# Gated linear attention and an FP4 MLP on one core: roots of norms taken on GpSimd, norms turned sooner, the causal mask selected

## The chip, the cores and the metric

The kernel runs on one core of a Trainium2 chip. A core has five engines that run side by side, each through its own list of instructions in order, and wait for one another on semaphores: TensorE (PE; its weight loads are listed apart as PEld), VectorE (DVE), ScalarE (ACT), GpSimd (POOL) and SyncE (SP), which here issues DMA transfers. The metric is the device time of the whole kernel in microseconds.

## The reference

Two pre-normed residual layers over x of 4 sequences x 512 tokens x 512 numbers:

```python
x = x + attn(layernorm(x), ...)     # gated linear attention, chunked
x = x + ffn(layernorm(x), ...)      # weights of 4 bits, 32 share a scale

def layernorm(x): return (x - mean) / sqrt(var + 1e-05)

# attn: 4 heads of 128, chunks of 128 tokens; q, k, v = x @ W + b
k = k / maximum(norm(k), 1e-12)
alpha, beta = sigmoid(x @ Walpha + balpha), softplus(x @ Wbeta + bbeta)
cla = cumsum(log(alpha + 1e-06))                    # within a chunk
decay = where(causal, exp(cla_i - cla_j), 0)
y_local = ((q @ k.T) * beta_j * decay) @ v
state = state * exp(cla_end) + (v.T @ (k * beta * exp(cla_end - cla)))
y = y_local + (q @ old state) * exp(cla)

# ffn: 512 -> 4096 -> 512
out = (gelu(x @ Wg.T) * (x @ Wu.T)) @ Wd.T
```

## The kernel before

**Tiling.** A tile is 128 tokens, which is one chunk; a sequence ("batch", b from 0 to 3) has four tiles (n from 0 to 3), so there are 16 chunks. `two_k` and `one_k` are lists of 24 and 42 fixed SBUF homes, taken and given back by name (`Homes`); PSUM has eight tiles of 128 x 512, used in rotation (`psum`).

**Order.** All is written out by hand (`manual_schedule`). The main loop (L858) goes through twelve products for each batch: four of v (`product_v`, a tile each), four of q (`product_q`, a head each), four of k (`product_k`, a tile each). After each product comes a *place*, numbered p, in which `behind(p)` (L656) issues the other work. Three places make a round for one chunk:

- p % 3 = 0: `chunk_lead` (k turned by TensorE, copied by ACT), `take_roots` (ACT's square roots of all that has been gathered), `gates_sums` once per batch, `chunk_decay`.
- p % 3 = 1: `settle` (what follows the roots on DVE), `chunk_scores`, `gates_end` once per batch, the load of the residual tile.
- p % 3 = 2: `turn` (normed tiles turned by TensorE and passed on), `gates_ln` once per batch, `chunk_sums`, and the statistics of a tile of the next batch (`first_norm`).

The chunk that a place works on is (p - 9) // 3, so chunks trail the k products. The second layer (`mlp`, a generator) goes through 35 rounds, i from 0 to 34, of 1 to 4 blocks of 128 hidden columns, batch i % 4 in turn. A block has two products of 12 matmuls (`gate_up`, L719); a round ends in `down` (L755), but for round 0, whose part is summed in round 4. Each product and each `down` is again followed by a place while attention is still going on; two of these stand between the k products of the last batch. So the last four chunks lie among the first rounds of the second layer. Round i with r = i - 3 has all four blocks from i = 3 on ("round zero", r = 0).

**A norm.** `norm` (L322) has DVE make statistics (L324, L326) and puts a root on a list. `take_roots` (L344) runs ACT's Sqrt. `settle` (L353) has DVE take the reciprocal (L331) and write the normed tile hn (L334). `turn` (L358) has TensorE transpose it (L362), and its `use` passes it on: of the first norm, ACT copies into hT (L373), from which all products read; of the second norm, ACT and DVE split it in three (L384 to L386), and SP stores the pieces in DRAM (h<-g, L388), from which each round of the second layer loads them (x<-h, L310 through `load_x`, twelve tiles per round). The second norm comes from `chunk_sums` (L646), so it passes three places from statistics to `turn`.

**k's norm.** `product_k` sums squares (ACT L448, DVE L450) and bounds them (L452); the root is again ACT's (L347); DVE takes the reciprocal (L456) and multiplies it with beta (brn, L458) and with beta and the decay to the end (kwf, L460). POOL scales v by brn (vb, L611) and k by kwf (kw, L607) in `chunk_scores`.

**Decay.** `chunk_decay` has TensorE spread a row of cla over 128 rows: `all_of` (48 x 128, ones at the rows of a chunk) times `rowsum` (48 x 512). pc (L558, if n > 0) is that alone; pm (L560) is the same with a second product added (L561) that puts -32768 where the mask is 0. ACT takes exp of pc (cd, L566), and of pm with cla_j subtracted, per head (dm, L577). POOL makes qc = q x cd (L568) and the decayed state (L585). TensorE makes scores sp (L595), DVE multiplies them into dm (L612). `chunk_sums` has TensorE add kw x v (dp, L624) to the state (DVE L626 or L628), and make yp from dm x vb (L637) and qc x old state (L639); DVE adds yp to the residual (L644).

**x of a round.** `load_x(i + 1, ...)` is issued in `last()` (L791), between the second product of a round's last block and what DVE does with it; for some rounds the first six of the twelve go out ahead, before the block numbers in `ahead` (L786): block 0 from i = 3 on, block 1 for i = 1, none for i = 2. SP's queue issues them in this order, behind the stores that they read from.

**Weights** of the second layer are unpacked on DVE and ACT (`dequant`), a step or two at a time from a queue (`unpack`), between the products.

## Time and profile before

| what | us |
|---|---|
| median of 3 runs | 1347.25 (1345.63 to 1349.15) |
| the profiled execution's own time | 1347.27 |
| its span, first to last instruction | 1345.5 |
| PE busy | 1318.1 |
| DVE, ACT, POOL busy | 983.8, 489.0, 62.0 |

In the profile, L12 is line 12 of the kernel before. `out<-in` are tiles by the program's names with numbers left out: tp_a and tp_f are the turned first and second norm, hn_a and hn_f the normed tiles. A busy time counts overlapping instructions once. "Idle <-" and the lists of waits name what an engine's wait ended on; a wait for several things is put down to the last. Matmuls are pipelined and listed with a modelled end, so the distance from one start to the next says what one costs.

### The profile page before, as it was taken

To read this page: it belongs to the slowest core of one execution; us is meant where nothing else is said; L and a number is where in the kernel's file an instruction comes from. 1 tells how busy PE (TensorE), PEld (TensorE's weight loads), DVE (VectorE), ACT (ScalarE), POOL (GpSimd) and SP (SyncE) were. 2 spreads that over 40 slices of the span, in tenths; PEclk is the share of its full clock that TensorE was granted. 3 is DMA by queue.
4 is the path that set the end of the run, shared out by engine and by line. 5 is a ranking of instruction groups with operands and counts; after the bars stand their busy time and mean duration, and the time that the engine had idled before them with its cause. 6 is when DMAs were issued, how large, how long until landed. Compare 5 with 4: busy or idle time off the path is not lost.

```text
span 1345.5 us, 17010 instructions
## 1 busy us (share of the span) xinstructions
PE 1318.1 (98%) x5828; PEld 1047.1 (78%) x5828; DVE 983.8 (73%) x1631; ACT 489.0 (36%) x855; POOL 62.0 (5%) x78
## 2 busy tenths in 40 slices
PE   8999999989999999999999999999999999999998
PEld 5576767676888888888888888888888888887886
DVE  4577766587767777777777777777778787777556
ACT  2554545544333333333333333333333333332232
POOL 0031313110000000000000000000000000000000
PEclk9999999999999999999999999999999999999999
DMA  7033334766555565556565656565656465555473
GB/s 235 24 99 105 103 94 132 264 199 213 187 164 194 176 194 180 191 181 199 177 199 185 194 178 206 185 195 173 201 175 206 156 216 172 189 172 188 149 254 129
DMA packets 173798, 236.57 MB, mean 176 GB/s; under 512 B 15760, under 2 KB 74128, under 8 KB 173712
## 3 DMA queue, kind: packets, MB, share of 16 engines
q1 hardware_dynamic: 173008, 235.20, 53.9%
q8 instruction: 46, 0.75, 0.2%
q10 hardware_dynamic: 704, 0.28, 0.1%
q14 instruction: 40, 0.33, 0.1%
HBM read 183.00 MB, written 52.43 MB: 175 GB/s over the span
## 4 chain that ended last, share of the span: by engine, by line
PE 89%; DVE 4%; ACT 3%; DMA 2%; issue 1%; POOL 1%; SPq 0%; POOLq 0%; DVEq 0%; ACTq 0%
PE pa L719 33%; PE p_d L755 25%; PE pb L719 16%; PE pq L428 4%; PE pva L403 2%; PE pvb L410 2%; PE pk L440 2%; DMA x<-h 1%; PE yp L637 1%; PE sp L595 1%; PE dp L624 1%; PE yp L639 1%; DMA h<-g 1%; ACT L349 0%; ACT sq L448 0%
## 5 line engine op out<-in xcount | busy, mean ns | idle before, releaser
L719 PE MATMUL pa<-x,wgu 128*128 128x512 f32 x2048 | 509.4, 390 | 0.9 <-DMA x<-h 0.7
L719 PEld LDWEIGHTS pa<-x,wgu 128*128 128x128 f32 x2048 | 385.1, 188 | 82.3 <-DMA x<-h 2.5
L755 PE MATMUL p_d<-wd,i 128*128 128x512 f32 x1536 | 358.3, 391 | 3.7 <-DVE i L740 2.5
L755 PEld LDWEIGHTS p_d<-wd,i 128*128 128x128 f32 x1536 | 288.7, 188 | 67.2 <-DVE i L740 3.5
L725 ACT ACTIVATE t<-pb 128x512 f32<-128x512 f32 x256 | 151.3, 591 | 352.6 <-PE pb L719 350.1
L719 PE MATMUL pb<-x,wgu 128*128 128x512 f32 x1024 | 275.0, 390 | 0.6 <-DMA x<-h 0.4
L726 DVE TENSOR_TENSOR t<-pa,t 128x512 f32<-128x512 f32 x256 | 176.5, 689 | 104.4 <-ACT t L725 99.1
L719 PEld LDWEIGHTS pb<-x,wgu 128*128 128x128 f32 x1024 | 192.3, 188 | 41.8 <-DMA x<-h 1.4
L768 DVE SCALAR_TENSOR_TENSOR acc<-p_d,acc 128x512 f32<-128x512 f32 x136 | 93.3, 686 | 109.3 <-PE p_d L755 102.0
L738 ACT ACTIVATE i<-t 128x512 fp32r<-128x512 f32 x128 | 81.0, 633 | 196.3 <-DVE t L735 194.8
L730 ACT ACTIVATE t<-t 128x512 f32<-128x512 f32 x128 | 81.1, 633 | 154.1 <-DVE t L726 154.1
L740 DVE TENSOR_TENSOR i<-t,i 128x512 fp32r<-128x512 f32 x128 | 88.2, 689 | 24.1 <-ACT i L738 22.6
L769 DVE TENSOR_TENSOR acc<-acc,p_d 128x512 f32<-128x512 f32 x136 | 93.6, 688 | 15.6 <-PE pa L719 1.4
L735 DVE SCALAR_TENSOR_TENSOR t<-t,t 128x512 f32<-128x512 f32 x128 | 88.6, 692 | 4.4
L741 DVE SCALAR_TENSOR_TENSOR i<-i,t 128x512 fp32r<-128x512 f32 x128 | 87.7, 685 | 0.2 <-DMA h<-g 0.2
L440 PE MATMUL pk<-wk,hT 128*128 128x512 f32 x128 | 57.6, 592 | 0.0
L428 PE MATMUL pq<-hT,wq 128*128 128x512 f32 x128 | 57.5, 593 | 0.0
L428 PEld LDWEIGHTS pq<-hT,wq 128*128 128x128 f32 x128 | 23.7, 190 | 23.9 <-issue 23.4
L440 PEld LDWEIGHTS pk<-wk,hT 128*128 128x128 f32 x128 | 23.5, 190 | 23.6 <-issue 23.4
L211 DVE SCALAR_TENSOR_TENSOR wgu<-wgu,w_gu 128x1024 fp32r<-128x1024 f32 x32 | 39.4, 1232 | 2.4 <-ACT wgu L208 2.4
L202 DVE SCALAR_TENSOR_TENSOR w_gu<-i_gu,sc_gu 128x1024 f32<-128x1024 f16 x32 | 39.7, 1240 | 0.0
L214 DVE TENSOR_TENSOR wgu<-wgu,wgu 128x1024 fp32r<-128x1024 f32 x32 | 39.5, 1234 | 0.0
(133 smaller groups left out, 911.6 us busy)
## 6 DMA issues: line engine op xcount, KB each, us to landing
x<-h SPq DMA_DIRECT2D x420, 256.0 KB
acc<-acc SPq DMA_DIRECT2D x256, 256.0 KB
h<-g SPq DMA_DIRECT2D x48, 256.0 KB
x<-in_x SPq DMA_DIRECT2D x16, 256.0 KB
pk_gu<-in_gate_p SPq DMA_DIRECT2D x32, 128.0 KB
sc_gu<-in_gate_s SPq DMA_DIRECT2D x64, 64.0 KB
pk_gu<-in_up_p SPq DMA_DIRECT2D x32, 128.0 KB
sc_gu<-in_up_s SPq DMA_DIRECT2D x64, 64.0 KB
```

Source lines behind the costliest of these rows:

```text
L428: nc.tensor.matmul(pq, f32(wq[k // 2])[:, k % 2, h * P : (h + 1) * P], f32(hT[b][k // 2])[:, k % 2, :], start=(k == 0), stop=(k == KC - 1),)
L440: nc.tensor.matmul(pk, f32(hT[b][k // 2])[:, k % 2, n * P : (n + 1) * P], f32(wk[k // 2])[:, k % 2, :], start=(k == 0), stop=(k == KC - 1),)
L719: nc.tensor.matmul(o, w3[j][:, k % 2, c * P : (c + 1) * P], x[j * KC + k], start=(j == js[0] and k == 0), stop=(j == js[-1] and k == KC - 1),)
L725: nc.scalar.activation(f32(t), pb, AF.Copy, scale=-1.0 / ONE_E)
L726: nc.vector.tensor_tensor(f32(t), pa, f32(t), ALU.add)
L730: nc.scalar.activation(f32(g), f32(g), AF.Gelu_apprx_tanh, scale=ONE_E)
L735: nc.vector.scalar_tensor_tensor(f32(u), f32(g), ONE_E, f32(u), ALU.mult, ALU.mult)
L740: nc.vector.tensor_tensor(il, f32(u), f32(ih), ALU.subtract)
L741: nc.vector.scalar_tensor_tensor(im, f32(ih), ONE_E, f32(u), ALU.mult, ALU.subtract)
L755: nc.tensor.matmul(o, inter[i][j][:, n * P : (n + 1) * P], wd[ms[i] // 2][j][:, ms[i] % 2, :], start=(i == 0 and j == js[0]), stop=(i == L ...
L768: nc.vector.scalar_tensor_tensor(a, pas[2 * n], ONE_E, a, ALU.mult, ALU.add)
L769: nc.vector.tensor_tensor(a, a, pas[2 * n + 1], ALU.subtract)
```

## The change

The roots move from ACT to POOL: a norm's variance plus 1e-5, and k's bounded sum of squares, are raised to the power -1/2 by a two-input POOL instruction whose second input is a tile of -0.5, which gives the reciprocal root at once. k's bound and the products brn and kwf go to POOL as well and follow in `product_k` itself. The list of roots and `take_roots` are gone, `settle` is called once, at the end of a place with p % 3 = 2, and no longer in the second layer's products. `turn` is told which norms to take: the second one's ("f") at p % 3 = 0 behind `chunk_decay`, the first one's ("a") at p % 3 = 1. kw and vb are issued at p % 3 = 0 (`chunk_values`).

The mask is no longer added by TensorE: ACT takes exp of pc for dm too (now ahead of cd), and POOL's `affine_select` writes 0 where j > i. `ident_r`, `neg` and `negm` are gone; `one_of_h`, `of_n`, `all_of`, `la`, `pieces` and `rowsum` have 128 rows, not 48. The state's sum on DVE goes behind the second norm's statistics. The warm-up on ACT is an Exp. Before round zero's x, six of its twelve tiles are issued ahead of block 2 of round i = 2.

```diff
@@ -132,7 +132,6 @@
     make_identity(nc, ident)
-    ident_r = const.tile([P, P], F32R, tag="ident_r", name="ident_r")
@@ -140,42 +139,29 @@
     )
-    home = one_k.get("neg")
-    neg = heads(f32(home))
-    nc.gpsimd.memset(neg, 0.0)
-    nc.gpsimd.affine_select(
-        out=neg, in_=neg, compare_op=ALU.is_ge, fill=-32768.0, base=0,
-        pattern=[[0, H], [1, P]], channel_multiplier=-1,
-    )
-    negm = const.tile([P, H, P], F32R, tag="negm", name="negm")
     ones = const.tile([P, P], F32, tag="ones", name="ones")
...
-    R2 = 32 + NCH * H
-    one_of_h = const.tile([R2, H], F32, tag="one_of_h", name="one_of_h")
-    of_n = const.tile([R2, 2, NCH], F32, tag="of_n", name="of_n")
-    all_of = const.tile([R2, NCH, P], F32R, tag="all_of", name="all_of")
-    eps_ln = const.tile([P, 1], F32, tag="eps_ln", name="eps_ln")
-    nc.gpsimd.memset(eps_ln, 1e-5)
+    one_of_h = const.tile([P, H], F32, tag="one_of_h", name="one_of_h")
+    of_n = const.tile([P, 2, NCH], F32, tag="of_n", name="of_n")
+    all_of = const.tile([P, NCH, P], F32R, tag="all_of", name="all_of")
+    minus_half = const.tile([P, H], F32, tag="minus_half", name="minus_half")
+    nc.gpsimd.memset(minus_half, -0.5)
     eps_la = const.tile([P, 1], F32, tag="eps_la", name="eps_la")
...
     def constants():
-        nc.vector.tensor_copy(ident_r, ident)
-        nc.vector.tensor_copy(negm, neg)
-        one_k.put(home)
         nc.vector.tensor_reduce(
-            one_of_h, ident[:R2, :R2].rearrange("p (n h) -> p h n", h=H), AX.X, ALU.add
+            one_of_h, ident.rearrange("p (n h) -> p h n", h=H), AX.X, ALU.add
         )
...
                 of_n[:, i, :],
-                ident[:R2, 32 * i : 32 * i + NCH * H].rearrange("p (n h) -> p n h", h=H), AX.X, ALU.add,
+                ident[:, 32 * i : 32 * i + NCH * H].rearrange("p (n h) -> p n h", h=H), AX.X, ALU.add,
             )
         nc.vector.tensor_tensor(of_n[:, 0, :], of_n[:, 0, :], of_n[:, 1, :], ALU.add)
-        nc.vector.tensor_copy(all_of, of_n[:, 0, :].unsqueeze(2).to_broadcast([R2, NCH, P]))
+        nc.vector.tensor_copy(all_of, of_n[:, 0, :].unsqueeze(2).to_broadcast([P, NCH, P]))
     def dequant(pk, sc, n, w3, key):
@@ -317,18 +303,18 @@
-    roots, settled, turned = [], [], []
+    settled, turned = [], []
     def norm(src, key, use):
...
         nc.vector.bn_aggr(mv, st)
-        sd = small.tile([P, 1], F32, tag="sd", name=f"sd_{key}")
+        rs = small.tile([P, 1], F32, tag="rs", name=f"rs_{key}")
+        nc.gpsimd.tensor_scalar(rs, mv[:, 1:2], 1e-5, None, ALU.add)
+        nc.gpsimd.tensor_tensor(rs, rs, minus_half[:, :1], ALU.pow)
         def settle():
-            rs = small.tile([P, 1], F32, tag="rs", name=f"rs_{key}")
-            nc.vector.reciprocal(rs, sd)
@@ -339,30 +325,22 @@
-        roots.append((sd, mv[:, 1:2], eps_ln, settle))
-    def take_roots():
-        for out_, in_, bias, then in roots:
-            if bias is None:
-                nc.scalar.activation(out_, in_, AF.Sqrt)
-            else:
-                nc.scalar.activation(out_, in_, AF.Sqrt, bias=bias)
-            settled.append(then)
-        roots.clear()
+        settled.append(settle)
     def settle():
...
-    def turn():
-        for hn, key, use in turned:
+    def turn(which):
+        for done in [t for t in turned if t[1][0] in which]:
+            turned.remove(done)
+            hn, key, use = done
             tp = psum(f"tp_{key}")
...
             use(tp)
-        turned.clear()
     def first_norm(b, n, src):
@@ -449,18 +427,13 @@
         one_k.put(sq)
-        nc.vector.tensor_scalar(sn, sn, 1e-24, None, ALU.max)
-        def settle():
-            rn = small.tile([P, H], F32, tag="rn", name=f"rn{b}_{n}")
-            nc.vector.reciprocal(rn, sn)
-            brn = small.tile([P, H], F32, tag="brn", name=f"brn{b}_{n}")
-            nc.vector.tensor_tensor(brn, rn, beta[b][:, n * H : (n + 1) * H], ALU.mult)
-            kwf = small.tile([P, H], F32, tag="kwf", name=f"kwf{b}_{n}")
-            nc.vector.tensor_tensor(kwf, rn, bdte[b][:, n * H : (n + 1) * H], ALU.mult)
-            ss[b, n] = brn, kwf
-        return lambda: roots.append((sn, sn, None, settle))
+        nc.gpsimd.tensor_scalar(sn, sn, 1e-24, None, ALU.max)
+        nc.gpsimd.tensor_tensor(sn, sn, minus_half, ALU.pow)
+        brn = small.tile([P, H], F32, tag="brn", name=f"brn{b}_{n}")
+        nc.gpsimd.tensor_tensor(brn, sn, beta[b][:, n * H : (n + 1) * H], ALU.mult)
+        kwf = small.tile([P, H], F32, tag="kwf", name=f"kwf{b}_{n}")
+        nc.gpsimd.tensor_tensor(kwf, sn, bdte[b][:, n * H : (n + 1) * H], ALU.mult)
+        ss[b, n] = brn, kwf
@@ -494,7 +467,7 @@
-        la = gate(b, "la", R2)
+        la = gate(b, "la", P)
         nc.gpsimd.memset(la, 0.0)
@@ -502,7 +475,7 @@
         nc.vector.reciprocal(dd, dd)
-        nc.vector.tensor_copy(la[:, 32:], la[:, :NG])
+        nc.vector.tensor_copy(la[:, 32 : 32 + NG], la[:, :NG])
         nc.vector.tensor_tensor(lw, lw, dd, ALU.mult)
@@ -517,17 +490,17 @@
         rps = psum(f"rps{b}")
-        nc.tensor.matmul(rps[:R2, :P], la, tri, start=True, stop=True)
-        pieces = gate_pool.tile([R2, P], F32R, tag="pieces", name=f"pieces{b}")
-        nc.scalar.activation(pieces, rps[:R2, :P], AF.Copy, scale=HI)
+        nc.tensor.matmul(rps[:, :P], la, tri, start=True, stop=True)
+        pieces = gate_pool.tile([P, P], F32R, tag="pieces", name=f"pieces{b}")
+        nc.scalar.activation(pieces, rps[:, :P], AF.Copy, scale=HI)
         ncla[b], bdte[b], td[b] = (gate(b, nm) for nm in ("ncla", "bdte", "td"))
...
         nc.vector.tensor_tensor(bdte[b], cps[:, NG : 2 * NG], ncla[b], ALU.add)
-        nc.vector.tensor_tensor(pieces[32:], rps[32:R2, :P], f32(pieces)[32:], ALU.subtract)
+        nc.vector.tensor_tensor(pieces[32:64], rps[32:64, :P], f32(pieces)[32:64], ALU.subtract)
         rowsum[b] = one_k.get(f"rowsum{b}")
         nc.vector.tensor_tensor(
-            heads(rowsum[b][:R2, :]), f32(pieces).unsqueeze(1).to_broadcast([R2, H, P]),
-            one_of_h.unsqueeze(2).to_broadcast([R2, H, P]), ALU.mult,
+            heads(rowsum[b]), f32(pieces).unsqueeze(1).to_broadcast([P, H, P]),
+            one_of_h.unsqueeze(2).to_broadcast([P, H, P]), ALU.mult,
         )
@@ -553,14 +526,22 @@
     def chunk_decay(b, n):
         toks = slice(n * P, (n + 1) * P)
-        pc = psum(f"pc_{b}_{n}") if n > 0 else None
-        if n > 0:
-            nc.tensor.matmul(pc, all_of[:, n, :], rowsum[b][:R2, :], start=True, stop=True)
-        pm = psum(f"pm_{b}_{n}")
-        nc.tensor.matmul(pm, all_of[:, n, :], rowsum[b][:R2, :], start=True, stop=False)
-        nc.tensor.matmul(pm, ident_r, negm.rearrange("p h c -> p (h c)"), start=False, stop=True)
+        pc = psum(f"pc_{b}_{n}")
+        nc.tensor.matmul(pc, all_of[:, n, :], rowsum[b], start=True, stop=True)
         if n == NCH - 1:
             one_k.put(rowsum[b])
+        dm = one_k.get(f"dm_{b}_{n}")
+        for h in range(H):
+            nc.scalar.activation(
+                f32(dm)[:, h * P : (h + 1) * P], pc[:, h * P : (h + 1) * P], AF.Exp,
+                bias=ncla[b][:, n * H + h : n * H + h + 1],
+            )
+        nc.gpsimd.affine_select(
+            out=heads(f32(dm)), in_=heads(f32(dm)), compare_op=ALU.is_ge, fill=0.0, base=0,
+            pattern=[[0, H], [1, P]], channel_multiplier=-1,
+        )
+        ch["dm"] = dm
         if n > 0:
@@ -571,14 +552,6 @@
             ch["qc"] = qc
-        dm = one_k.get(f"dm_{b}_{n}")
-        for h in range(H):
-            nc.scalar.activation(
-                f32(dm)[:, h * P : (h + 1) * P], pm[:, h * P : (h + 1) * P], AF.Exp,
-                bias=ncla[b][:, n * H + h : n * H + h + 1],
-            )
-        ch["dm"] = dm
         if n + 1 < NCH:
@@ -587,19 +560,8 @@
-    def chunk_scores(b, n):
-        toks = slice(n * P, (n + 1) * P)
...
+    def chunk_values(b, n):
         brn, kwf = ss.pop((b, n))
@@ -609,8 +571,22 @@
         nc.gpsimd.tensor_tensor(heads(f32(vb)), heads(f32(v_sb[b, n])), bc(brn), ALU.mult)
+        ch["vb"] = vb
+    def chunk_scores(b, n):
+        toks = slice(n * P, (n + 1) * P)
...
         nc.vector.tensor_tensor(f32(dm), sp, f32(dm), ALU.mult)
-        ch["vb"] = vb
     def chunk_sums(b, n):
@@ -622,10 +598,6 @@
                 nc.tensor.matmul(dp[:, hs], f32(kw)[:, hs], f32(v)[:, hs], start=True, stop=True)
-            if n == 0:
-                nc.vector.tensor_copy(f32(new), dp)
-            else:
-                nc.vector.tensor_tensor(f32(new), f32(new), dp, ALU.add)
             state[b] = new
@@ -644,6 +616,10 @@
         second_norm(b, n, a)
+        if n == 0:
+            nc.vector.tensor_copy(f32(new), dp)
+        elif n + 1 < NCH:
+            nc.vector.tensor_tensor(f32(new), f32(new), dp, ALU.add)
@@ -662,15 +638,16 @@
                 chunk_lead(cb, n)
-            take_roots()
+                chunk_values(cb, n)
             if first and j == 6:
...
                 chunk_decay(cb, n)
+            turn("f")
             if exps:
...
         elif p % 3 == 1:
-            settle()
+            turn("a")
             if chunk:
@@ -682,13 +659,13 @@
         else:
-            turn()
             if first and j == 5:
...
                 first_norm(*t, xs.pop(t))
+            settle()
@@ -720,7 +697,6 @@
                         )
-            settle()
             t = one_k.get(f"t{i}_{key}")
@@ -783,7 +759,7 @@
             a4 = residual(i) if i > 0 else None
-            ahead = [0] if i >= B - 1 else [1] if i == 1 else []
+            ahead = [0] if i >= B - 1 else [i] if i > 0 else []
             for q, mt in enumerate(ms):
@@ -828,14 +804,13 @@
-        warm = small.tile([P, 1], F32, tag="sd", name="warm")
-        nc.scalar.activation(warm, eps_ln, AF.Sqrt)
+        warm = small.tile([P, 1], F32, tag="warm", name="warm")
+        nc.scalar.activation(warm, eps_la, AF.Exp)
         for c in range(KC // 2):
...
             nc.sync.dma_start(wvb_[:, 2 * c : 2 * c + 2, :VB], rows(Wv, c)[:, :, VA:])
-        nc.gpsimd.tensor_copy(wvb_[:, :, VB:], wab_sb)
         x0 += [load(tile_of(n), f"x0_{n}") for n in range(2, NCH)]
@@ -846,23 +821,22 @@
         def first(n):
             first_norm(0, n, x0[n])
-            take_roots()
             settle()
         first(0)
+        nc.gpsimd.tensor_copy(wvb_[:, :, VB:], wab_sb)
         constants()
-        turn()
+        turn("a")
         first(1)
...
             for j in range(3 * NCH):
-                later = None
                 if j < NCH:
...
                         def between():
-                            turn()
+                            turn("a")
                             if j + 2 < NCH:
@@ -872,7 +846,7 @@
                 else:
-                    later = product_k(b, j - 2 * NCH)
+                    product_k(b, j - 2 * NCH)
                 if b == B - 1:
@@ -885,8 +859,6 @@
                 behind(p)
-                if later:
-                    later()
                 if p in (5, 7):
```

## The prediction

> **What bounds the kernel now.** I read the page first (busy shares, the slices, the chain), then stretches of the span, then TensorE's waits, then the timeline where it waits.
>
> ```profile
> PE 1318.1 (98%) x5828; PEld 1047.1 (78%) x5828; DVE 983.8 (73%) x1631; ACT 489.0 (36%) x855; POOL 62.0 (5%) x78
> ...
> PE 89%; DVE 4%; ACT 3%; DMA 2%; issue 1%; POOL 1%; SPq 0%; POOLq 0%; DVEq 0%; ACTq 0%
> ```
>
> TensorE is busy nearly always and carries 89% of the chain. So time is won by giving TensorE less to do or by closing its gaps, and the next view says where these are (columns: stretch, length, busy time of PE, PEld, DVE, ACT, POOL, granted clock, DMA share, GB/s).
>
> ```profile
> 0.00:20.00 20.00, 13.62 (x56) 11.27 (x57) 9.23 (x30) 4.41 (x12) 2.66 (x15) 1.00 0.89 301
> 20.00:260.00 240.00, 236.35 (x1067) 158.05 (x1065) 155.97 (x388) 119.25 (x249) 47.83 (x50) 1.00 0.38 115
> 260.00:340.00 80.00, 69.98 (x324) 53.89 (x323) 58.41 (x102) 39.74 (x66) 11.46 (x13) 0.96 0.66 215
> 340.00:1220.00 880.00, 880.00 (x3884) 728.66 (x3883) 679.35 (x994) 290.38 (x471) 0.00 (x0) 1.00 0.57 184
> 1220.00:1346.00 126.00, 118.12 (x505) 95.19 (x503) 80.87 (x120) 35.26 (x57) 0.00 (x0) 0.98 0.54 192
> ```
>
> From 340 on there is only the second layer: no idle TensorE until 1220, no POOL, and no line of the change. Everything it can do lies before 340: in the attention part (20 to 260, PE idle for 3.65 of 240) and in the overlap with the first rounds of the second layer (260 to 340, PE idle for 10.0, clock 0.96). What TensorE waits for there:
>
> ```profile
> PE dp L624 <- POOL kw L607: 5.1, 4, 2.8
> PE tp_f L362 <- DVE hn_f L334: 3.6, 1, 3.6
> ...
> PE yp L637 <- POOL vb L611: 1.1, 2, 0.8
> PE sp L595 <- ACT kT L550: 0.8, 1, 0.8
> PE pa L719 <- DMA x<-h: 0.7, 3, 0.3
> PE yp L637 <- DVE dm L612: 0.6, 1, 0.6
> ```
>
> Each is a late product of the norms' roots or of ScalarE's queue, but for the x loads. Last, one chunk's decay products on TensorE, and the longest gap:
>
> ```profile
> 80.33 0.60 PE L547 MATMUL tpk<-ident,k 128*128 128x128 f32 x4
> 80.86 0.49 PE L558 MATMUL pc<-rowsum,all_of 48*128 48x512 f32 x1
> 81.20 0.39 PE L560 MATMUL pm<-rowsum,all_of 48*128 48x512 f32 x1
> 81.52 0.50 PE L561 MATMUL pm<-negm,ident_r 128*128 128x512 f32 x1
> 81.86 1.45 PE L428 MATMUL pq<-hT,wq 128*128 128x512 f32 x3
> ```
>
> ```profile
> 265.52 1.08 PE L719 MATMUL pb<-x,wgu 128*128 128x512 f32 x4
> 270.22 0.66 PE L362 MATMUL tp_f<-ident,hn_f 128*128 128x128 f32 x4 [3.62 <-DVE hn_f L334]
> ```
>
> Read starts, not lengths: matmuls overlap, so one costs the distance to the next start (pc 0.34, pm 0.32, mask 0.34).
>
> **The change, part by part.** Sums are made against the profiled execution, 1347.27 us (span 1345.5, 1.8 around it); the median of the runs shown is 1347.25, so nothing has to be shifted.
>
> *Mask off TensorE.* In the 12 chunks with n > 0, three products (81.86 - 80.86 = 1.00) become one (0.34): 12 x 0.66 = 7.9. In the four with n = 0, the pair (113.22 to 113.98, 0.76) becomes one: 4 x 0.42 = 1.7. Together **9.6 us** of TensorE work, in a stretch where it is 98% busy and DVE 65%, ACT 50%. Its stationary side grows from 48 to 128 rows; the row with 128 (L561, 0.34) is no dearer than those with 48, so I put nothing down; bounds are 0.11 less for each of the 16 (the second layer's 128-row products step 0.227) and 0.1 more.
> It adds a POOL select per chunk: L147's on the same 128x512 took 0.64. The dm it masks is wanted by DVE a place later (products q and k step 3.4, second-layer ones 2.7). ACT now does the four decay exponentials (1.14 a chunk) ahead of cd's, not behind it (0.60). So pc + 1.5 + 0.64 and some hand-overs, about 2.5, against 3.4: hidden. If that cover went, it would be up to 0.64 x 16 = 10. Behind the select on POOL wait qc (1.42) and the state's decay (1.04), wanted two places on.
>
> *Roots to POOL.* ACT loses 32 roots of 0.29, 16 of 0.19 and at least the 18 table loads of 1.28 before them (13 on L349, 5 on L347), some 23 us of loads, and many loads back to Exp. DVE loses two reciprocals of 0.157 per tile, and per chunk L452, L456, L458 and L460 (0.173, 0.167, 0.374, 0.187): 16 x 1.2 = 19 us. Neither engine bounds, so that alone gives nothing; what it gives is earlier results. POOL gains 10 us of selects and some 130 small instructions; its 62 us lie in 310, so it stays idle for most. The trace has no power. From below, a POOL instruction on 128x1 is 0.10 (L161); from above, the dearest row POOL has, two inputs on 128x512, is 1.24. I take 0.3, the same root of the same 128x1 on ACT (0.29), which is nearest in what it computes.
> The Trainium skill (ScalarE: Activation LUTs, section What ACT_TABLE_LOAD costs) prices a switch at about 1.28 us of load and 1.38 of drain. Here the load at 246.54 took 1.28 and the root began at 247.84, so no drain is seen; by the page ACT would gain twice as much, and the sum the same.
> The first tile's chain (mv_a ready 4.66, hn_a begun 5.23) trades 0.57 of root and reciprocal for an add (0.10), a power and two hand-overs: 0 at 0.3, 0.9 later at 1.24.
> The page GPSIMD Engine Reference of the skill (section 2.1, Instruction dispatch) speaks against this: the first call of a freshly loaded POOL routine pays about 6 us with nothing shown in the profile. No row here shows whether a power is such a call; by that rule the start, and the sum, would be 6 us later.
>
> *Keys' factors and values on POOL, one place sooner.* kw and vb no longer wait for ACT's root, DVE's queue and the place of the scores; their factors come from POOL itself, behind the square and its sum. In the first chunk of batches 0, 1, 2 TensorE's starts show 0.7, 1.9 and 2.5 us lost around tp_f, dp and yp (at 57, 122 to 125, 188 to 192): **5.1 us** go.
>
> *The overlap, 260 to 340.* Steps against starts: tp_f at 270.22, 3.8 (above); sp at 281.44 behind kT, 1.0; dp at 288.64 behind kw, 3.0, and then 24 small products at a lowered clock until 292.97, 1.6; yp at 307.72 behind dm, 0.8; the down product from 320.99 (36 x 0.227 = 8.2, took 9.4), 1.2; and 20 products from 330.38 to 340.40 that should take 4.5, 5.5 lost to x<-h and the clock behind it. Together 16.9. The last: h<-g of the last tile is issued at 322.93, since its tp_f is at 317.79; then SP issues twelve x<-h, 6.22 for all, from 325.35. After, tp_f comes two places sooner (about 312.4), h<-g at least 5 us sooner, and six x loads go out a product ahead; behind them on SP stand only a weight fetch and the other six. So that stall goes; were h<-g still late, 5.5 would stay.
> What is late next: the turned norm. DVE now makes hn_f right behind the chunk's sum, waiting for POOL, and TensorE wants it one product, tpk and pc later. In the attention part, chunk 1: yp ends 76.99, sum, statistics and aggregate 1.6, so 78.7; meanwhile DVE does the state's add and the next norm's statistics until 80.1; hn_f (0.55) is done at 80.7, tp_f is wanted at 81.2. Add and power may take 1.8 before TensorE waits. In the overlap there is no such slack: DVE comes free late. Chunk 13: free at 275.6, aggregate 277.1, power 277.6, hn_f 278.3, wanted 277.0: 1.3. Chunk 12 likewise 1.0, chunk 15 1.1; chunk 14 is followed by a 5.6 us down product: none. That is 3.4 back, and I leave 1.8 for sp and yp, whose wait is DVE's and ACT's order. Of 16.9, **11.7** remain. The state's add is put behind the norm, and no one needs it before the next chunk's yp.
> The turn's other work moves with it: ACT's g (0.58) queues behind cd and ahead of the gates' two exponentials and the next product's copy, DVE's pair (2 x 0.68) ahead of the next product's sums instead of ahead of the chunk's own, and SP's three h<-g (0.6 each) ahead of the x loads as before. Where tp_f is late by 1, these are too; eight PSUM tiles stand between them and TensorE.
>
> *At nothing.* Constants: POOL drops 1.2 us of fills, DVE two casts (0.64) behind the first hn_a, while TensorE transposes; wider reductions add some 0.1 there. The copy of Wab's columns (0.21, at 3.95) goes behind POOL's add and power; pvb reads it at 12.0. If the power took 6 us there, pvb would wait. The warm-up loads another table in the same idle ACT. Norms of the second to fourth tile have a product (3.7) of cover.
>
> Sum: 9.6 + 5.1 + 11.7 = 26.4, so 1347.3 - 26.4 = **1321 us**.
>
> **Rivals.**
> *All gaps close* (no new norm waits): 9.6 + 5.1 + 16.9 = 31.6, 1316; with the 128-row products at 0.227, 1314. For it: DVE is lighter by 1.2 a chunk. Against: chunk 13's numbers above.
> *DVE becomes the overlap's bound.* It is busy for 58.4 of 80; less 4 for four chunks is 54, and 17 less on the clock leaves 63, or 86%. If half of 16.9 goes and 3.4 comes back, the gain is 9.6 + 5.1 + 5.0 = 19.7, 1328; if nothing is won there, 1336; a select that isn't hidden ends at the same place (10 given back, 1331). Against: from 340 on DVE is at 77% with no PE gap.
> *Slower: the power is dear.* hn_f waits for it on DVE, and TensorE for hn_f at the next turn. Beyond 1.6 us each further us costs 12 in the attention part, and each us above 0.3 costs 3 in the overlap: at 2.9 it costs 15.6 + 7.8 = 23 and the gain is nearly gone; from about 3.1 on it is slower; at 5 it costs 41 + 14, 1376. For it: the 1.24 is another operation's row, so nothing shown forbids 3. Against: in that time POOL handles 512 elements of each partition, and here it has one or four.
> *The gain is hidden*: TensorE's 9.6 turn into waits of the same chunks for dm or hn_f, 0.6 each, and the overlap's gaps only move: 1343 to 1347.
>
> **How the numbers follow.** Forecast 0.58 (1317 to 1327), all gaps close 0.12, DVE-bound overlap 0.17, hidden 0.04, slower 0.09. A measurement of this kernel tells 0.3% (4 us) from no change. Faster 0.87, same 0.04, slower 0.09. The range leaves out the slower and the hidden case and the far ends: 1313 to 1336.
>
> **What would show it.** One pc per chunk on TensorE and no pm; POOL selects of about 0.64; power rows of 0.3 (up to 1.2 changes little, 3 turns it); no table load ahead of roots; dp and yp without waits for kw and vb; TensorE's waits for hn_f of about 1 us at three turns of the overlap; no x<-h wait at the round of 330; the stretch from then to the end as long as before. I am wrong if waits for hn_f stand at every chunk, or if the second layer's tail changes.

## The result, and the profile after

The changed kernel takes 1331.62 us (median of 4 runs, 1330.86 to 1333.14) against 1347.34 (4 runs, 1345.63 to 1349.15): a ratio of 0.9885 [0.9867, 0.9902]. That is 15.7 us of the 26.4 forecast. The profiled execution took 1330.86 us and its span is 1329.1, so 1.8 lies around it, as before, and the working below is in its span.

In the page, busy time and the chain; in the answer by stretches, the same columns as before:

```profile
PE 1299.9 (98%) x5800; PEld 1041.1 (78%) x5800; DVE 974.8 (73%) x1533; ACT 441.8 (33%) x777; POOL 123.9 (9%) x220
...
PE 89%; DVE 4%; POOL 2%; ACT 2%; issue 2%; DMA 1%; POOLq 0%; ACTq 0%; DVEq 0%
```

```profile
20.00:260.00 240.00, 234.26 (x1097) 161.43 (x1096) 156.68 (x324) 87.07 (x198) 108.13 (x182) 1.00 0.40 123
260.00:340.00 80.00, 70.48 (x336) 58.16 (x336) 62.63 (x93) 32.21 (x54) 11.10 (x18) 0.98 0.72 235
340.00:1210.00 870.00, 870.00 (x3840) 720.39 (x3839) 671.37 (x983) 285.02 (x462) 0.00 (x0) 1.00 0.56 183
```

TensorE has 28 products fewer (5828 to 5800: two in each of twelve chunks, one in four) and still carries 89% of the chain. POOL's part of the chain grows from 1% to 2%, and what is new is 5.74 us of idle TensorE from 20 to 260, where it was 3.65. The waits of TensorE say for what:

```profile
PE tp_f L341 <- DVE hn_f L320: 9.2, 6, 3.0
PE tp_a L341 <- DVE hn_a L320: 7.4, 2, 6.1
PE yp L609 <- DVE dm L589: 4.3, 3, 3.5
```

The waits for kw, vb and x are gone. In their place the turned second norm is waited for six times, 9.2 us in all. (Of tp_a's 7.4, 6.1 are the program's start.)

Where the time came from is read from one and the same product in both traces, after minus before, in us:

| product | shift |
|---|---|
| first v product of batch 0 | +0.2 |
| first q product of batch 0 | +2.0 |
| first v product of batch 1 | +0.2 |
| first v product of batch 2 | -4.9 |
| first v product of batch 3 | -10.1 |
| last k product (249.4) | -10.0 |
| round that waited for x (330 before) | -10.7 at its start, -16.2 behind it |
| last instruction | -16.4 |

The forecast, at the same places: 12.7 by the last k product (the mask's 9.6 less three chunks of 0.66 that come later, and 5.1), 13.7 from there to 340 (those three chunks and 11.7), nothing in the tail. So the attention part gave 10.0 of 12.7, the overlap 6.2 of 13.7, and the tail, with 0.2, nothing.

### The profile page after: what moved, and what is told of

Read it like the earlier page. It is cut to its first block, busy times and chain, and to the rows that moved or that the text cites. A ratio compares the mean times of both kernels' runs of the same rounds, so it can differ in the third digit from the quotient of the medians.

```text
span 1329.1 us, 16898 instructions
## 1 busy us (share of the span) xinstructions
PE 1299.9 (98%) x5800; PEld 1041.1 (78%) x5800; DVE 974.8 (73%) x1533; ACT 441.8 (33%) x777; POOL 123.9 (9%) x220
## 4 chain that ended last, share of the span: by engine, by line
PE 89%; DVE 4%; POOL 2%; ACT 2%; issue 2%; DMA 1%; POOLq 0%; ACTq 0%; DVEq 0%
PE pa L696 34%; PE p_d L731 25%; PE pb L696 17%; PE pq L406 4%; PE pva L381 2%; PE pvb L388 2%; PE pk L418 1%; PE sp L581 1%; PE tp_a L341 0%; ACT sq L426 0%; POOL ss L431 0%; PE yp L611 0%; PE yp L609 0%; PE tp_f L341 0%; DVE t L702 0%
```

## The experiments

Line numbers are those of the changed kernel unless the text says otherwise. Where two versions are compared, the ratio to the kernel before on each one's own chip is used: a difference of 0.001 is 1.35 us.

Beside the ratio stands the distance of the traces at 340, since two things that no edit touches differ between the profiled executions. Both are the clock that TensorE was granted (the number before the last two). In the tail, from 1200 to 1260, it is 0.97 in the kernel before and the changed one and 1.00 in e2, e3, e8 and e11, whose tails are some 1.5 us shorter. In the overlap it differs too (the changed kernel, e3, e8, e12):

```profile
240.00:340.00 100.00, 88.58 (x428) 71.18 (x427) 75.33 (x114) 41.46 (x70) 22.24 (x34) 0.98 0.75 246
240.00:340.00 100.00, 90.00 (x418) 71.49 (x417) 75.04 (x114) 40.20 (x67) 20.80 (x32) 0.95 0.73 241
240.00:340.00 100.00, 91.59 (x416) 71.46 (x415) 75.74 (x114) 41.05 (x69) 21.71 (x32) 0.95 0.76 244
240.00:340.00 100.00, 85.96 (x402) 68.62 (x401) 78.44 (x119) 38.95 (x65) 22.66 (x34) 0.95 0.70 232
```

The loss comes in pieces: in e3 the clock is 0.50 from 264 to 269, and eight products of one kind take longer there than in the changed kernel at full clock (second row):

```profile
264.89 3.76 PE L696 MATMUL pa<-x,wgu 128*128 128x512 f32 x8
...
259.76 2.09 PE L696 MATMUL pa<-x,wgu 128*128 128x512 f32 x8
```

Up to 346 the changed kernel has 3.4 us at half clock, and e3, e5, e8, e12 and e13 have 10.2. By the longer steps of TensorE's products in them that costs 1.3 us there and 3.5 to 4.4 us here (an estimate). No run shows what brings these stretches, so a lead that is lost in the overlap need not all be DVE's doing.

**e1: the second norm turned one place later.**

```diff
             if chunk:
                 chunk_decay(cb, n)
-            turn("f")
...
         elif p % 3 == 1:
-            turn("a")
+            turn(("a", "f"))
```

> The second norm's tiles are turned one place later (p % 3 = 1, with the first norm's), all else as in the changed kernel. Theory A (the turn comes too soon for DVE): the six waits of TensorE for hn_f, 9.2 us by the list of waits and 10.2 by the distances of starts, are gone, and with no other loss the time is 1331.6 - 10 = 1321 to 1323. Rival B (the waits only move: h<-g and the three DVE and ACT steps behind the turn come a place later and hold up the scores, the homes or round zero's x): 1329 to 1333.

Measured: 1327.33 us (1327.19 to 1328.66), ratio 0.9849 [0.9834, 0.9863], 4.9 us better than the change itself. TensorE's waits:

```profile
PE yp L609 <- DVE dm L589: 5.1, 4, 3.4
...
PE sp L581 <- ACT kT L523: 1.9, 1, 1.9
...
PE tp_f L341 <- DVE hn_f L320: 0.4, 1, 0.4
```

The 9.2 us for hn_f are all but gone (0.4), so the turn is what waited. But only about half came out as time, between the two expectations: a wait for kT of 1.9 and 0.8 more for dm are new, and in the round that the x loads feed a lead of 5.3 us over the change falls to 3.6, where it stays.

**e2: the root left out.** Both powers become products with the same tile, so the norms are not normed: an output without roots, to price the power in its place.

```diff
-        nc.gpsimd.tensor_tensor(rs, rs, minus_half[:, :1], ALU.pow)
+        nc.gpsimd.tensor_tensor(rs, rs, minus_half[:, :1], ALU.mult)
...
-        nc.gpsimd.tensor_tensor(sn, sn, minus_half, ALU.pow)
+        nc.gpsimd.tensor_tensor(sn, sn, minus_half, ALU.mult)
```

> Both powers on POOL become products by -0.5 on the same tiles, so the roots are left out of the computation and only their price goes: 0.58 to some 0.2 on 128x1, 1.11 to some 0.2 on 128x4. Theory A (DVE is late with the norm's sum, and the root adds little): each of the six waits for hn_f shrinks by 0.4, in chunks 3 by up to 0.9 more where POOL does k's factors first; 1331.6 - 2 to 4 = 1328 to 1330. Rival C (the dear power, 0.58 and 0.23 for the add where 0.3 and 0.1 were put, makes the waits): they are nearly gone, 1321 to 1324.

Measured: 1324.47 us (1323.96 to 1325.61), ratio 0.9826 [0.9812, 0.9841], 7.9 us better by the ratios, but 4.3 in the trace from 340 on (1.5 of the rest is the tail's clock). POOL's groups of the changed kernel, then of e2 (busy us, mean ns of one, idle before):

```profile
L431 POOL TENSOR_TENSOR ss<-ss,minus_half 128x4 f32<-128x4 f32 x16 | 17.8, 1110 | 1.3
...
L315 POOL TENSOR_TENSOR rs_f<-rs_f,minus_half 128x1 f32<-128x1 f32 x16 | 9.2, 573 | 1.3
...
L314 POOL TENSOR_SCALAR rs_f<-mv_f 128x1 f32<-128x1 f32 x16 | 3.6, 227 | 73.8 <-DVE mv_f L312 73.3
```

```profile
L431 POOL TENSOR_TENSOR ss<-ss,minus_half 128x4 f32<-128x4 f32 x16 | 3.2, 200 | 1.3
...
L315 POOL TENSOR_TENSOR rs_f<-rs_f,minus_half 128x1 f32<-128x1 f32 x16 | 3.0, 189 | 1.3
```

A power costs 0.57 on 128x1 and 1.11 on 128x4, the product in the same place 0.19 and 0.20. TensorE's wait for hn_f falls from 9.2 to 5.4, not to nothing, with the power down to 0.19, below the 0.3 forecast. So the price of the two powers (k's stands ahead of the norm's on POOL) is a good part of the missing gain: 4.3 us. Of the 5.4 that are left, DVE's order, the hand-overs and the longer hn_f are not told apart.

**e3: batch 0's first norms turned apart from batch 1's.** In the fourth v product of batch 0, `turn("a")` also finds batch 1's first tile, which has only just been normed (TensorE waits 1.25 at 24).

```diff
-        for done in [t for t in turned if t[1][0] in which]:
+        for done in [t for t in turned if t[1].startswith(which)]:
...
                         def between():
-                            turn("a")
+                            turn("a0")
```

> Inside the first four v products only tiles of batch 0 are turned; so the first tile of batch 1 is turned at its place, not in the middle of the fourth v product. Theory A: the wait of 1.25 for hn_a at 25.1 us is gone and nothing takes its place: 1.4 less, 1330.2. Rival: the first q products have slack enough that later waits take it up again: 1331.6.

Measured: 1329.28 us (1328.58 to 1330.21), ratio 0.9863 [0.9845, 0.9881]. In the trace it is 2.3 us ahead through the whole attention part, and 0.7 ahead from 306 on: the stretches at half clock from 263 and 301 on cost 2.7 and 1.6, and two waits of the down product on DVE (xr 1.0, state 0.8) another 1.6, while the wait for dm at 274 is 2.8 shorter. The medians' difference (3.0 by the ratios) holds 1.5 us of the tail, where nothing was edited and the clock differs; the trace's 0.7 is the part that has a cause.

**e4: two x tiles fewer sent ahead in round 1.** The second gap of the overlap, 3.5 us at 274, is a wait of yp for dm. In the timeline of the changed kernel, it goes back to an ACT instruction that waited for a store:

```profile
275.79 0.60 ACT L701 ACTIVATE t<-pb 128x512 f32<-128x512 f32 x1 [3.39 <-DMA h<-g]
276.42 0.69 DVE L702 TENSOR_TENSOR t<-pa,t 128x512 f32<-128x512 f32 x1 [2.70 <-ACT t L701]
277.02 0.68 DVE L589 TENSOR_TENSOR dm<-sp,dm 128x512 f32<-128x512 f32 x1
```

By the order in which the program gives out its SBUF tiles, this t gets the home of a piece of g, whose store is still reading it; six x tiles loaded ahead hold the other homes.

```diff
-                    load_x(i + 1, jk[:6])
+                    load_x(i + 1, jk[: 4 if i == 1 else 6])
```

> Four, not six, x tiles go ahead in round 1, so that the t of that round's last block takes a home that was read long ago instead of one from which a store (h<-g) is still reading. Theory D: ACT's t at 275.8 us no longer waits 3.4 us for the store, the DVE step dm behind it comes at least 2 us sooner, and TensorE's wait of 3.5 for it falls to about 1: 2 to 3.5 less, 1328 to 1329.6. Rival (DVE's order alone makes dm late, or x of round 2 comes late): 1331 to 1333.

Measured: 1329.64 us (1329.38 to 1330.73), ratio 0.9865 [0.985, 0.988]. ACT's t now waits 0.8 us for the store, the waits for dm fall from 4.3 to 1.1, and the program is 4.0 us ahead at the down product that follows (some 1.0 of it because the changed kernel is at half clock just there). There it waits for DVE instead (xr 1.3, state 0.8), and from 340 on it is 1.6 ahead. So the home was the cause of that gap, and DVE is what stands behind it. (In e3 and e5 the waits for dm are as short, 1.5 and 1.2, though t waits 3.4 and 3.1 for the store as before: there TensorE comes later itself, at half clock.)

**e5: 48 rows again** in all_of and rowsum (and the tiles they are made from), the rest as changed.

```diff
-    all_of = const.tile([P, NCH, P], F32R, tag="all_of", name="all_of")
+    all_of = const.tile([R2, NCH, P], F32R, tag="all_of", name="all_of")
...
-        nc.tensor.matmul(pc, all_of[:, n, :], rowsum[b], start=True, stop=True)
+        nc.tensor.matmul(pc, all_of[:, n, :], rowsum[b][:R2, :], start=True, stop=True)
```

> The changed kernel with the row products' tiles back at 48 rows (one_of_h, of_n, all_of, la, pieces, rowsum). Theory F (a matmul whose stationary side has 128 rows starts sooner behind the transposes: tpk to pc was 0.53 before and is 0.36 after, pc to the next 0.34 and 0.32): 16 x 0.19 = 3.0 more TensorE time, less what the chunks that wait for hn_f swallow (6 of 16), so 2 to 3 more, 1333.5 to 1334.6. Rival (the shorter distance has another cause, such as the missing second product): 1331.6.

Measured: 1334.88 us (1332.96 to 1335.97), ratio 0.9901 [0.9887, 0.9916]: 2.2 us dearer by the ratios, 3.9 by the traces' distance from 340 on. From pc's start to the next it is 0.43 with 48 rows and 0.32 with 128; from the transposes ahead to pc it is 0.53 and 0.36. By the last k product, with the same clock in both, e5 is 2.7 us behind; the 1.2 more of the overlap come with a clock of 0.95 against 0.98. The part that I had put at nothing is worth some 2.7 us up to there.

**e6: the mask alone.** The kernel before, with one pc for both exponentials and the select on POOL; roots, turns and kw stay as they were.

```diff
-        pc = psum(f"pc_{b}_{n}") if n > 0 else None
-        if n > 0:
-            nc.tensor.matmul(pc, all_of[:, n, :], rowsum[b][:R2, :], start=True, stop=True)
-        pm = psum(f"pm_{b}_{n}")
-        nc.tensor.matmul(pm, all_of[:, n, :], rowsum[b][:R2, :], start=True, stop=False)
-        nc.tensor.matmul(pm, ident_r, negm.rearrange("p h c -> p (h c)"), start=False, stop=True)
+        pc = psum(f"pc_{b}_{n}")
+        nc.tensor.matmul(pc, all_of[:, n, :], rowsum[b][:R2, :], start=True, stop=True)
...
+        nc.gpsimd.affine_select(
+            out=heads(f32(dm)), in_=heads(f32(dm)), compare_op=ALU.is_ge, fill=0.0, base=0,
+            pattern=[[0, H], [1, P]], channel_multiplier=-1,
+        )
```

> The kernel before with one part of the change alone: the mask by POOL's select and one row product per chunk, with 48 rows; roots, norms and turns as before. Theory A: TensorE loses 9.6 us of work at the trace's distances, the waits of before stay, the select is hidden: 1347.8 - 9 to 10 = 1338 to 1339; in the overlap some of it may be taken up again (1340). Rival (the 9.6 hides behind dm, which now waits for POOL, or behind late norms): 1344 to 1348.

Measured: 1348.9 us (10 runs, 1346.93 to 1351.03) against 1347.61 (13 runs): ratio 1.001 [1.0001, 1.0019]. The products are gone (the steps of pc and pm sum to 6.8 us, 15.0 before), and nothing is won. TensorE's waits (line numbers of the kernel before):

```profile
PE dp L624 <- POOL kw L607: 6.6, 7, 3.2
...
PE tp_f L362 <- DVE hn_f L334: 5.2, 3, 4.7
...
PE yp L637 <- DVE dm L612: 1.7, 1, 1.7
```

With kw still issued a place later, it now stands behind the select on POOL, and dp waits for it seven times. Taken alone, the mask's 8.2 us turn into other losses: at the first product of the second layer e6 is still 2.1 us ahead, from 346 on 0.1. By the lists the waits grow by 4.5 in all (kw 1.5, hn_f 1.6, dm 1.1, vb 0.3), and from 240 to 340 the granted clock is 0.93, where it was 0.97. So the mask needs some of the other parts to be won. That it is kw and vb a place sooner is likely, but was not run apart.

**e7: no x loads ahead in round 2**, as in the kernel before.

```diff
-            ahead = [0] if i >= B - 1 else [i] if i > 0 else []
+            ahead = [0] if i >= B - 1 else [1] if i == 1 else []
```

> The changed kernel without the six x tiles sent ahead in round 2. Theory G (in the changed kernel SP sends all twelve in one run from 307.0 us anyway, because the last h<-g is issued at 304.5; what took the wait away is the sooner turn): 0 to 1 more, 1331.6 to 1332.6. Rival (sending ahead is what took it away): the 4 to 5.5 us come back, 1335.6 to 1337.

Measured: 1331.93 us (1330.72 to 1332.13), ratio 0.9878 [0.9862, 0.9895]: the same (in the trace it is 1.1 behind from 340 on). The stall for x does not come back, so the loads sent ahead had no part in it. What is left is the sooner turn, and with it the sooner store of g: the last h<-g is issued at 304.48 in the changed kernel and at 322.93 before.

**e8: e1, e3 and e4 together.**

```diff
+        for done in [t for t in turned if t[1].startswith(which)]:
...
-            turn("f")
...
+            turn(("a", "f"))
...
+                    load_x(i + 1, jk[: 4 if i == 1 else 6])
...
+                            turn("a0")
```

> The three edits together: second norms turned one place later, only batch 0 turned inside the first v products, four x tiles ahead in round 1. If they were independent, the medians add: 1331.6 - 4.3 - 2.3 - 2.0 = 1323. Theory E (from 250 to 320 us DVE's queue is what is late, and a wait that is taken away returns at the next thing that DVE owes TensorE, such as the PSUM tiles that the down product waits for): 1325 to 1328, with waits of TensorE for DVE in that stretch still above 3 us.

Measured: 1326.93 us (1325.65 to 1327.55), ratio 0.9843 [0.9828, 0.9857], 5.7 us better than the change. Alone the three gave 4.9, 3.0 and 2.7; together no more than e1 and a little. By the traces at 340 it is 3.6, 0.7 and 1.6 alone and 2.9 together. There the lead over the change is 7.3 us at the start of the down product at 280.6, 5.0 thirteen products later, 4.5 at 320 and 3.0 behind the round that the x loads feed. TensorE's waits in the overlap are now on other DVE and ACT work:

```profile
PE yp L609 <- DVE dm L589: 3.1, 3, 1.5
...
PE p_d L730 <- DVE xr L616: 1.9, 1, 1.9
PE sp L581 <- ACT kT L523: 1.9, 1, 1.9
```

With them come some 2.4 us more lost at half clock than in the changed kernel, so how much of the lost lead is DVE's is not shown.

**e9: a dearer root.** Two more powers, with exponent 1.0, for each norm; they take 0.55 each, and with the hand-overs the way from the add to the last power is 2.15 us, where it was 0.88: 1.26 more for each root.

```diff
         nc.gpsimd.tensor_tensor(rs, rs, minus_half[:, :1], ALU.pow)
+        nc.gpsimd.tensor_tensor(rs, rs, ones[:, :1], ALU.pow)
+        nc.gpsimd.tensor_tensor(rs, rs, ones[:, :1], ALU.pow)
```

> The changed kernel with two more powers (by 1.0) behind each norm's root, so the way over POOL is 1.15 us longer for every tile. By the prediction's terms (slack for a power of 1.6 in the attention part, none in the overlap): power 1.73, so 12 x 0.13 + 3 x 1.15 and 1.15 at the first tile: 6 more, 1337.8. By the trace after (the attention part has at most 0.5 left at the turns without a wait, and none at the four with one): 12 x 0.65 to 1.15, 3 x 1.15 and 1.15 at the start, 12 to 18 more: 1344 to 1350, the whole gain.

Measured: 1362.85 us (1361.27 to 1364.57), ratio 1.0115 [1.0091, 1.0139], 31 us slower than the change: 25 us for each us of root, and far above the expected 1344 to 1350.

```profile
PE tp_f L343 <- DVE hn_f L322: 24.3, 15, 4.3
PE tp_a L343 <- DVE hn_a L322: 12.0, 4, 7.5
```

Fifteen of sixteen turns now wait. Two things were left out of the expectation: the first norms beyond the first tile, by which 6.0 us are lost by the first scores already, and the granted clock, 0.98 from 20 to 240 and 0.95 from 240 to 340 (1.00 and 0.98 in the changed kernel). A straight line gives an estimate of the break-even: the 15.7 us are used up by a root 15.7 / 25 = 0.6 us dearer. Since the first part of a dearer root is still partly hidden, it may be somewhat more.

**e11: hn_f written by POOL**, to take 16 instructions of 0.55 to 1.26 off DVE.

```diff
-            nc.vector.tensor_scalar(
+            (nc.gpsimd if key[0] == "f" else nc.vector).tensor_scalar(
```

> The changed kernel with the normed tile of the second norm (hn_f) written by POOL, right behind its power, and not by DVE; the first norm's stay on DVE. DVE loses 16 x 0.76 and the 6.4 us that it stood waiting for POOL; POOL's step over 128x512 should take 0.7 to 1.1 against 0.55 to 1.26. Theory E (DVE's queue is what is late from 250 to 320): waits of TensorE for DVE fall in that stretch, 2 to 5 less, 1327 to 1329.6. Rival (POOL's longer step, and kw and vb behind it, make the turn and the sums as late): 1331 to 1334.

Measured: 1364.18 us (1358.22 to 1365.26), ratio 1.0118 [1.009, 1.0146].

```profile
L320 POOL TENSOR_SCALAR hn_f<-xr,mv_f,rs_f 128x512 f32<-128x512 f32 x16 | 36.5, 2283 | 0.9
```

On POOL the step takes 2.28 us, not the expected 0.7 to 1.1, and TensorE waits for it 34.5 us at 15 turns. DVE's relief is worth nothing against that.

**e12: 12 needless DVE sums**, 0.81 us busy each, at places 46 to 57 (the overlap).

```diff
     def behind(p):
+        if 46 <= p < 58:
+            whole = f32(all_of).rearrange("p n c -> p (n c)")
+            nc.vector.tensor_tensor(scratch, whole, whole, ALU.add)
```

> The changed kernel with one more DVE instruction of 0.69 us (a sum of 128x512 that nobody reads) at each of the twelve places 46 to 57, 8.3 us in all, in the overlap alone. Theory E (DVE bounds the overlap): most of it comes out as time, 4 to 8 more, 1335.6 to 1340. Rival (DVE has room there, 57 of 80 us busy, and single late steps make the waits): under 2 more, 1331.6 to 1333.6.

Measured: 1336.04 us (1335.03 to 1336.27), ratio 0.9917 [0.9899, 0.9934]: 4.3 us by the ratios, 5.4 in the trace from 340 on, of 9.7 us put in. About half of what DVE is given in the overlap comes out as time, some 3 us of it at half clock. So DVE has little room there, though its busy share is 78% (62.63 of 80); that it alone sets the pace is not shown.

**e13: e8, and the add of eps on DVE**, right behind the aggregate.

```diff
-        nc.gpsimd.tensor_scalar(rs, mv[:, 1:2], 1e-5, None, ALU.add)
+        nc.vector.tensor_scalar(rs, mv[:, 1:2], 1e-5, None, ALU.add)
```

> The three edits of e8 (turn for the feed-forward one place later, each batch's first norm turned with its own batch, four x tiles ahead in round 1), and the add of eps back on DVE, right behind the aggregate, so that of the root only the power is left on GpSimd. In the trace of after the add takes 0.23 to 0.31 on GpSimd with a hand-over ahead of it, and on DVE an instruction on 128x1 takes some 0.06 to 0.1: each norm is some 0.2 us sooner, where nothing else holds DVE. Theory E (in the overlap DVE sets the pace and the norms' trip is no longer what TensorE waits for once the turn is a place later): nothing to be seen, 1326 to 1328, against 1326.9 for e8. Theory L (the trip of the norm is still wanted): 18 norms by 0.2 that TensorE would gain directly, at most 3.6, so 1323 to 1326, with fewer waits of p_d and yp. Rival: the add stands in DVE's order behind a wait and holds other DVE work: 1328 to 1331.

Measured: 1324.82 us (5 runs, 1323.73 to 1327.2), ratio 0.9835 [0.9821, 0.9848], the lowest median of the kernels that compute all. Against e8 the intervals overlap. The trace says 1.05 us sooner by 122 and 0.9 from 340 on: less than the 3.6 of the one theory, though the median lies in its range, and more than the nothing of the other. On DVE the add took 0.15, not the 0.06 to 0.1 I had expected.

## Why the prediction was right or wrong

**What bounds, and where.** Right: all 16.2 us come before 340, and the tail is as long as before. The signs named in advance came, too: 16 pc and no pm, 16 table loads on ACT where there were 45, and waits for hn_f that are new but don't stand at every chunk (six turns). The time lies in the stated range, but only because that reaches up to 1336 for the rivals: the forecast's own 1317 to 1327 is missed by 4.6 us. And part of that is luck, since 2.7 us came from a term that the sum had at nothing.

**Mask, 9.6.** The work went as forecast, and the select (0.86 on average, L540) is hidden: none of TensorE's three waits for dm goes back to it. "Its stationary side grows from 48 to 128 rows ... I put nothing down" was wrong to the good side: e5 gives 2.7 us by the last k product, more than the bound of 0.11 a chunk (1.8 in all), since pc starts sooner behind the transposes too. And e6 shows what the sum didn't say: by itself the term brings nothing. The rival "gain hidden" is what the mask does by itself.

**First chunks of a batch, 5.1.** The waits of dp and yp for kw and vb are gone. But at the same chunks new ones stand, for hn_f: 0.3, 0.8, 2.0 and 1.6 at 64, 126, 187 and 247, together 4.7. And 1.4 at 24 (e3) was not foreseen at all.

**The failed step: what is late next.** "Add and power may take 1.8 before TensorE waits" was read from chunk 1 and used for the whole attention part. Chunk 1 bears it out. In the timeline (start, duration; in brackets the idle time before and what ended it) chunk 1 comes first, then chunk 8, where TensorE waits, then chunk 13:

```profile
78.16 0.18 DVE L312 BATCH_NORM_AGGREGATE mv_f<-st_f 128x2 f32<-128x6 f32 x1
...
79.65 0.52 DVE L320 TENSOR_SCALAR hn_f<-xr,mv_f,rs_f 128x512 f32<-128x512 f32 x1
...
80.69 0.60 PE L341 MATMUL tp_f<-ident,hn_f 128*128 128x128 f32 x4
...
183.92 0.63 ACT L426 ACTIVATE sq<-k 128x512 f32<-128x512 f32 x1 [2.55 <-DVE k L424]
184.58 0.69 DVE L428 TENSOR_REDUCE ss<-sq 128x4 f32<-128x512 f32 x1 [0.70 <-ACT sq L426]
185.19 0.68 DVE L616 TENSOR_TENSOR xr<-xr,yp 128x512 f32<-128x512 f32 x1
...
185.67 1.04 POOL L431 TENSOR_TENSOR ss<-ss,minus_half 128x4 f32<-128x4 f32 x1
...
186.63 0.18 DVE L312 BATCH_NORM_AGGREGATE mv_f<-st_f 128x2 f32<-128x6 f32 x1
...
187.54 0.58 POOL L315 TENSOR_TENSOR rs_f<-rs_f,minus_half 128x1 f32<-128x1 f32 x1
188.09 1.04 POOL L569 TENSOR_TENSOR kw<-k,kwf 128x512 f32<-128x512 f32 x1
188.15 1.26 DVE L320 TENSOR_SCALAR hn_f<-xr,mv_f,rs_f 128x512 f32<-128x512 f32 x1 [0.77 <-POOL rs_f L315]
...
189.56 0.63 PE L341 MATMUL tp_f<-ident,hn_f 128*128 128x128 f32 x4 [1.82 <-DVE hn_f L320]
...
262.42 0.68 DVE L616 TENSOR_TENSOR xr<-xr,yp 128x512 f32<-128x512 f32 x1
...
263.86 0.18 DVE L312 BATCH_NORM_AGGREGATE mv_f<-st_f 128x2 f32<-128x6 f32 x1
...
264.13 0.24 POOL L314 TENSOR_SCALAR rs_f<-mv_f 128x1 f32<-128x1 f32 x1 [3.62 <-DVE mv_f L312]
264.45 0.58 POOL L315 TENSOR_TENSOR rs_f<-rs_f,minus_half 128x1 f32<-128x1 f32 x1
265.00 1.04 POOL L569 TENSOR_TENSOR kw<-k,kwf 128x512 f32<-128x512 f32 x1
265.06 1.26 DVE L320 TENSOR_SCALAR hn_f<-xr,mv_f,rs_f 128x512 f32<-128x512 f32 x1 [0.43 <-POOL rs_f L315]
...
266.47 0.63 PE L341 MATMUL tp_f<-ident,hn_f 128*128 128x128 f32 x4 [3.03 <-DVE hn_f L320]
```

In chunk 1, 0.5 us lie between hn_f's end and tp_f's start, and 0.5 to 0.6 in chunks 2, 5 and 6; but only 0.1 to 0.2 in chunks 3, 7, 9, 10 and 11, which is no slack, since the turns that did wait started as close behind hn_f. Chunk 8 has a k product in the same place, as every first chunk of a batch has (the last ones have one too). Its sum of squares holds DVE (it waits for ACT's square), so the chunk's own sum xr begins 1.6 us after yp's last product ended at 183.55. Its power of 1.04 with brn and kwf is on POOL until 187.1, ahead of this norm's. And hn_f takes 1.26, not 0.55.

In the overlap the same three sizes were off: chunk 13's wait was forecast at 1.3 and is 3.2. From the end of the aggregate to the end of the power is 1.0, where 0.5 was put (power 0.58 for 0.3, add 0.24 for 0.10, hand-overs); hn_f 1.26, where 0.7 was put. The remaining 0.8 is DVE coming to xr late.

**The overlap, 11.7.** 3.4 of waits for hn_f and 1.8 for sp and yp were to come back. Measured: hn_f 5.5 (at 263 and 300), yp for dm 4.8, of which 3.65 at 274 is the home of e4, and 0.9 in a down product: 11.2. The 6.0 more are most of the 7.5 that this stretch is short of; 1.5 I can't place. (Of the 0.9, 0.4 is a wait for the state's add, which by the prediction no one needs before the next chunk's yp. Of the 3.4, the 1.0 for chunk 12 falls at 247, ahead of the last k product, where 1.6 was measured.) The x stall of 5.5 went as forecast; its stated cause was half right, since the loads sent ahead had no part in it (e7).

**The sum.** In the attention part: 12.7, less 2.0 by the first q product, less 4.7 for hn_f, plus 2.7 for the 128 rows (e5 at the last k product), gives 8.7. The trace has 10.0, so 1.3 of gain are there that no term of mine accounts for.

**Rivals.** "Power dear" did not decide, but its price was: I put 15 us to each us of root from a threshold of 1.6 on, e9 shows 25 from where it stands, and a break-even near a power of 1.2 us by a straight line, not 3.1. "DVE becomes the overlap's bound" (1328) is nearest to what happened: e12 charges about half of DVE's extra work, and e3, e4 and e8 win time early that DVE's waits, the lower clock and, in e8, the x loads take back. The argument for the gaps closing, "DVE is lighter by 1.2 a chunk", added durations of small instructions that overlap and left out that hn waits for POOL more often: DVE's busy time fell by 9.0 us (983.8 to 974.8), not by 19.

**The first call.** The Trainium skill's page GPSIMD Engine Reference (section 2.1, Instruction dispatch) puts some 6 us on the first call of a freshly loaded routine. Here the first power took 0.57 (at 4.90), and the first v product starts 0.2 later than before; whether a power is a call of that kind, no row shows.

**Left open.** How the three parts of a late hn_f (power, POOL's order, the longer hn_f) share the 9.2 us, beyond e2's 3.8 for the powers. What brings the stretches at half clock. kw and vb issued behind hn_f, so that they don't meet, was not tried.

## What to carry to other kernels

A slack read from one iteration holds for iterations that have the same neighbours; read it again at the first and last ones of a batch and wherever two loops overlap, since there the queue ahead is another. A row of the kernel before can already show it: its hn_f at 268.81 took 1.36 us, not 0.55. When a root moves to another engine, price the whole trip from the last statistic to the first use (here add, power, two hand-overs, the engine's order), and ask what else the new engine starts the moment it is done. And gains of fixes in one stretch need not add: three that were worth 4.9, 3.0 and 2.7 us alone gave 5.7 together. Before the rest is put down to an engine, compare the granted clock of the runs.

## What the runs showed of the hardware that was not expected

**A normed tile on DVE waits for POOL.** In the changed kernel hn_f and hn_a take 0.51 to 0.55 us on DVE in 21 of 32 cases and 1.25 to 1.27 in 11. In every one of the 11, a POOL kw or vb over 128x512 had begun 0.06 or 0.07 earlier, and hn ended 0.28 or 0.29 after that POOL instruction did. Behind the small POOL adds and powers it keeps its 0.55. The kernel before has six such cases already (1.01 to 1.36) and e6 six (0.67 to 1.36), with POOL's state, kw or select begun between 0.43 earlier and 0.04 later, and hn again ended 0.28 after it. So in these 23 rows hn isn't slowed in proportion, it waits for POOL's end. e11 has eight rows of another kind: there hn_a, beside POOL's hn_f, took 1.03 and ended 1.05 or more before it. First the kernel before, then e11:

```profile
268.81 1.36 DVE L334 TENSOR_SCALAR hn_f<-xr,mv_f,rs_f 128x512 f32<-128x512 f32 x1
268.84 1.04 POOL L607 TENSOR_TENSOR kw<-k,kwf 128x512 f32<-128x512 f32 x1 [0.52 <-DVE rs_f L331]
...
155.00 2.12 POOL L320 TENSOR_SCALAR hn_f<-xr,mv_f,rs_f 128x512 f32<-128x512 f32 x1
155.04 1.03 DVE L320 TENSOR_SCALAR hn_a<-x,mv_a,rs_a 128x512 f32<-128x512 f32 x1 [0.99 <-POOL rs_a L315]
```

The change makes them meet more often: POOL's power releases hn, and POOL's next instruction, kw, begins just ahead of it. The skill's page SBUF — State Buffer (section SBUF: two separate sides) says that DVE and GpSimd share a port pair as an exclusive lock, held for the whole instruction by whichever starts first; on DVE's side it names instructions in a two-port mode or with two SBUF inputs. Of the 23 rows 21 agree, at 0.7 us for each meeting in the changed kernel; in two (268.81 above and its like in e6) hn's start stands 0.03 or 0.04 ahead of POOL's, and it waited all the same. The eight of e11 do not, and no row says which mode hn runs in.

**POOL prices.** A power is 0.57 on 128x1 and 1.11 on 128x4 (a product 0.19 and 0.20). hn_f, with two operands of one value per partition over 128x512, is 2.28 on POOL against 0.55 on DVE.

**48 rows are no cheaper than 128.** With a stationary side of 48 rows, pc starts 0.20 behind the last transposition ahead of it and the next product 0.43 behind pc (e5); with 128 rows it is 0.03 and 0.32. The rows alone don't decide: in the kernel before, the products with 48 rows step 0.34 (pc) and 0.32 (pm behind it), and 0.42 or 0.43 only where a pm comes straight behind the transpositions.
